# Two 3x3 convolutions by four products for two pixels, in a float32 stack of four layers with scans beside it

## The chip, the core and the metric

The kernel runs on one core of one Trainium2 chip, in one launch, in float32 throughout. The metric is the device time of one execution in microseconds (us). The profile is one execution taken by the hardware profiler; its engines are PE (TensorE matmul), PEld (its weight load), DVE (VectorE), ACT (ScalarE), POOL (GpSimd) and SP (SyncE, which issues all transfers here).

## What is computed

Eight images of 256 channels and 32 x 32 pixels go through four layers of the form x = x + layer(group_norm(x)), with a parameter-free group norm over 32 groups:

```
x = x + attention(gn(x))                      # 8 heads of 64, q and k of length one, projection
x = x + conv3x3(gn(x), s * sign_weights) + b1 # 256 -> 256 channels, padding 1
x = x + conv3x3(gn(x), weights) + b2          # 256 -> 256 channels, padding 1
x = x + layer3(gn(x))
```

Layer 3 is long: a layer norm, four branches of a selective scan (64 channels each, 128 inner channels, 16 states, 1024 tokens), a gate, depthwise convolutions along the tokens with pointwise ones after them, a second attention (8 heads of 32, "mixer attention"), a layer norm with gelu, a depthwise 3x3 convolution, another layer norm and a projection.

The change concerns the two 3x3 convolutions: out[o, h, w] is the sum over c, dy, dx of weight[o, c, dy, dx] times in[c, h + dy - 1, w + dx - 1].

## The kernel before

**Tiles.** An image is held as two tiles of 128 channels by 1024 pixels. A matmul takes 128 input channels by up to 512 pixels, and writes 512 float32 columns of PSUM. A float32 matmul appears in the profile as two records.

**Stages of one image.** `front_attention` (L576) is the first layer's attention; `front_convs` (L750) has its output projection and then the two convolutions; `scan_layers` (L1000) is the scan of layer 3; `back_layers` (L1151) has the layers up to and with the mixer attention; `back_out` (L1237) and `back_end` (L1263) close the image.

**The convolution.** `conv3x3` (L716) takes the statistics of the group norm (`group_stats`, L256, a chain of small operations between TensorE and VectorE), writes the normalised image into two tiles of 34 x 34 pixels with a border of zeros (`im`, by ScalarE), and for each of two output tiles m runs over input tile c, row dy, column dx and the two halves of the image: 36 matmuls into one PSUM tile of 1024 columns, each reading a shifted window of `im`. The weights come from memory in 12 chunks of 192 KB a convolution, through a pool of six buffers (`wsp`). One VectorE operation (`evac_1`, L763, or `evac_2`, L770) adds the PSUM tile to `xt`, and `channel_stats` (L249) takes the statistics for the next norm.

**The scan.** `scan_steps` (L885) works in 64 units an image: 4 branches, 2 halves of the tokens, 4 groups of states, 2 groups of channels. A unit has a product on GpSimd (`drive`, L929, tile `hs`), two exponentials on ScalarE into PSUM (`decays`, L933, tile `da`), two scans on VectorE (`scan`, L943), a second product on GpSimd (`weigh`, L958), and after each second unit eight records of small matmuls that add up the result (`add_up`, L965, tile `y`): I call two units that end so a pair, 32 an image. Before each branch, `branch_front` (L784) makes the branch's inputs, with TensorE, ScalarE, VectorE and a round trip through memory; `branch_back` (L857) closes it.

**The order.** [...]The order is written out by hand. Iteration b of the main loop has a *dense* stream, made of the back layers of image b-1 and the front layers of image b+1, and the *scans* of image b. Each stream is a generator that yields costs, planned TensorE time; `interleave` (L1335) adds up the dense costs, and takes one step of the scans (two steps are a unit) each time that a due time is reached, which then moves on by a pace:

```
spent += cost or 0.0
while scans is not None and due <= spent:
    due += pace
    with held():
        if next(scans, END) is END:
...
PACE = [1.8] + [2.95] * (batch - 2) + [1.6]
```

`Paced` (L93) and `held` (L118) tie each scan instruction to the last dense one of its engine, so that this order holds. `slow` (L1358) multiplies the costs of the front attention by 0.35, so few scan steps fall beside it. In the middle iterations the dense stream is: back layers with the mixer attention, output projections, front attention, then the convolutions of image b+1 with the closing layers of image b-1 between their steps (`amid`, L1348). Image 0's front layers stand alone ahead of the loop, and the last image's back layers alone behind it.

Of the kernel before, what the change touches and what calls it, by code (L numbers as in the profile page):

```python
# [2 lines left out]

# [1 line left out]

# [6 lines left out]
F32 = mybir.dt.float32  # L12
I32 = mybir.dt.int32
AF = mybir.ActivationFunctionType
ALU = mybir.AluOpType
# [4 lines left out]
P = 128  # L20
C = 256
N = 1024
HALF = 512
HALVES = (slice(0, HALF), slice(HALF, N))
NKT = N // P
TW = 34 * 34
NB, DM, DS, DTR = 4, 64, 16, 4


# [4 lines left out]
def preact_stack(ctx: ExitStack, tc: tile.TileContext, I, out, cols):  # L34
# [23 lines left out]
    ps_da = ctx.enter_context(tc.tile_pool(name="ps_da", bufs=2, space=PSUM))  # L58
    ps_y = ctx.enter_context(tc.tile_pool(name="ps_y", bufs=1, space=PSUM))
    dp = ctx.enter_context(tc.tile_pool(name="dp", bufs=2, space=DRAM))  # L60
    xdp = ctx.enter_context(tc.tile_pool(name="xdp", bufs=3, space=DRAM))

    def work(name):
# [5 lines left out]
    def big_tile():  # L69
        return ps_big.tile([P, N], F32, tag="big", name="big")  # L70
# [147 lines left out]
        half_qb, vec[:, cols["qpwb"] : cols["qpwb"] + 2], 0.5  # L218
    )


    images = [wp.tile([P, TW], F32, name="im%d" % t) for t in range(2)]
    raw = wp.tile([P, N + 4], F32, name="raw")
    for t in images + [raw]:
        nc.gpsimd.memset(t, 0.0)
# [19 lines left out]
    def stats_tile():  # L245

        return sp.tile([P, 2, 2], F32, tag="mv", name="mv", bufs=4)
# [8 lines left out]
    def group_stats(mv, psum):  # L256

        with urgent():
            pg = psum()
            tensor.matmul(  # L260
                pg[:, 0:4], gmat, mv.rearrange("p a b -> p (a b)"), start=True, stop=True
            )
            g = sp.tile([P, 2, 2], F32, tag="g", name="g", bufs=4)
            vector.tensor_copy(g.rearrange("p a b -> p (a b)"), pg[:, 0:4])
            d = sp.tile([P, 2], F32, tag="d", name="d")
            vector.tensor_sub(d, mv[:, :, 0], g[:, :, 0])
            vector.tensor_mul(d, d, d)
            pd = psum()
            tensor.matmul(pd[:, 0:2], gmat, d, start=True, stop=True)
            rs = sp.tile([P, 2], F32, tag="rs", name="rs", bufs=4)  # L270
            vector.scalar_tensor_tensor(
                rs, pd[:, 0:2], 1e-5, g[:, :, 1], ALU.add, ALU.add
            )
            inverse_root(rs)
            shift = sp.tile([P, 2], F32, tag="shift", name="shift", bufs=4)
            vector.scalar_tensor_tensor(
                shift, g[:, :, 0], -1.0, rs, ALU.mult, ALU.mult
            )
        return rs, shift

    def group_norm(xt, stats, dsts, view=lambda a: a):
        with urgent():
            scale, shift = stats
            for t in range(2):
                scalar.activation(
                    dsts[t],
                    view(xt[:, t]),
                    AF.Identity,
                    bias=shift[:, t : t + 1],
                    scale=scale[:, t : t + 1],  # L290
                )
# [421 lines left out]
    def image(a):  # L713
        return a.rearrange("p (h w) -> p h w", w=32)

    def conv3x3(xt, mv, name, bname, evac):  # L716


        im = [t.rearrange("p (h w) -> p h w", w=34) for t in images]
        group_norm(  # L720
            xt, group_stats(mv, acc_tile), [t[:, 1:33, 1:33] for t in im], image
        )
        mv = stats_tile()
        for m in range(2):
            scalar.activation(xt[:, m], xt[:, m], AF.Identity, bias=col(bname, m))
        yield 1
        for m in range(2):
            ps = big_tile()
            n = 0
            for c in range(2):  # L730
                for dy in range(3):
                    w = chunk(name, (m * 2 + c) * 3 + dy)
                    for dx in range(3):
                        for h in range(2):
                            tensor.matmul(
                                image(ps[:, HALVES[h]]),
                                w[:, dx],
                                im[c][:, 16 * h + dy : 16 * h + dy + 16, dx : dx + 32],
                                start=n == 0,
                                stop=n == 17,  # L740
                            )
                        n += 1
                    if n < 18:
                        yield 5.2
            evac(m, ps)
            channel_stats(mv, m, xt[:, m])
            yield 5.2
        return mv

    def front_convs(img):  # L750

        xt, o = img["x"], img.pop("o")
        mv = stats_tile()

        def evac_out(m, ps):
            vector.scalar_tensor_tensor(
                xt[:, m], ps, col("b_out", m), xt[:, m], ALU.add, ALU.add
            )
            channel_stats(mv, m, xt[:, m])

        yield from project_both("wout", o, evac_out)

        def evac_1(m, ps):  # L763
            vector.scalar_tensor_tensor(
                xt[:, m], ps, col("s1", m), xt[:, m], ALU.mult, ALU.add
            )

        mv = yield from conv3x3(xt, mv, "wc1", "b1", evac_1)

        def evac_2(m, ps):  # L770
            vector.tensor_add(xt[:, m], xt[:, m], ps)

        img["mv"] = yield from conv3x3(xt, mv, "wc2", "b2", evac_2)

# [580 lines left out]
            yield cost  # L1355
        yield from other

    def slow(stream):  # L1358

        for cost in stream:  # L1360
            yield SLOW * cost

    SLOW = 0.35
    PACE = [1.8] + [2.95] * (batch - 2) + [1.6]
    imgs = [{} for _ in range(batch)]
    drain(front_attention(image_of(0), imgs[0]), front_convs(imgs[0]))
    for b in range(batch):

        def dense():
            last = imgs[b - 1] if b > 0 else None  # L1370
            front = None
            if b + 1 < batch:
                front = front_attention(image_of(b + 1), imgs[b + 1])
            if last is None:
                yield from front
                yield from front_convs(imgs[b + 1])
                return
            for n, cost in enumerate(back_layers(last, begin=front)):
                yield cost
                if n == 2 and front is not None:  # L1380
                    next(front)
            if front is None:
                yield from back_out(last)
                yield from back_end(last, out[b - 1])
                return
            yield from islice(front, 4)
            ending = back_out(last)
            yield from islice(ending, 2)
            yield next(front)
            yield from ending  # L1390
            yield from slow(front)
            yield from amid(
                front_convs(imgs[b + 1]),
                back_end(last, out[b - 1]),
                (0, 4, 6, 7, 8, 9, 10, 11, 12, 13, 14, 16, 17, 20, 22, 25),
            )

        interleave(dense(), scan_layers(imgs[b]), PACE[b])
    last = imgs[batch - 1]
# [131 lines left out]
```

## Time and profile before

The time is 6625.64 us, the median of three (6609.48 to 6631.33). The profiled execution has a span of 6630.4 us.

| stretch | from, to (us) | what runs |
|---|---|---|
| image 0's front | 0 to 395 | attention, then two convolutions, no scans |
| iteration 0 | 395 to 1007 | front of image 1, scans of image 0 |
| iterations 1 to 6 | 1007 to 5668, about 777 each | back of b-1, front of b+1, scans of b |
| iteration 7 | 5668 to 6298 | back of image 6, scans of image 7 |
| the end | 6298 to 6630 | back of image 7 |

Costliest groups of instructions, with the mean time of a single record:

| engine, what | records | busy us | mean ns |
|---|---|---|---|
| PE, values of both attentions (acc<-p,v) | 4096 | 1189.7 | 653 |
| PE, the convolutions (big<-im,w) | 2304 | 1073.7 | 622 |
| POOL, drive (hs<-du,bc) | 512 | 1319.8 | 2594 |
| POOL, weigh (hs<-hs,bc) | 512 | 1278.8 | 2498 |
| DVE, scans | 1024 | 1228.2 | 1207 to 1268 |
| DVE, sums of the front attention (p<-p) | 448 | 717.0 | 1600 |

A row of groups reads: line, engine, operation, written tile <- read tiles, shapes, count | busy time, mean of one | idle time of the engine just before, and what ended most of it. Matmuls are pipelined, so the mean of one record is longer than what each adds to the engine's busy time. The line is mostly that of a helper (L101), so that groups are told apart by their tiles.

### The profile page before, as it was taken

What the parts mean: (1) busy time and instruction counts of PE and PEld (TensorE: products, weight loads), DVE (VectorE), ACT (ScalarE), POOL (GpSimd) and SP (SyncE); (2) the same over time, 40 slices, a digit from 0 to 9 for tenths busy, and PEclk for the clock granted to TensorE, in tenths of its full rate; (3) what the DMA queues carried; (4) which work ended last, traced back from release to release, by engine and by line L of the source; (5) the groups of instructions that cost most, each with busy time, mean ns of one, the idle gap of its engine ahead of it and who ended that gap; (6) DMA issues with size and microseconds to landing.
All of it is one profiled execution on the core that took longest, in us unless ns stands there. A gap on an engine that the chain in (4) does not pass through costs nothing.

```text
span 6630.4 us, 52730 instructions
## 1 busy us (share of the span) xinstructions
PE 5708.6 (86%) x17602; PEld 1926.6 (29%) x17602; DVE 3903.6 (59%) x4613; ACT 2687.2 (41%) x3225; POOL 2684.8 (40%) x1295
## 2 busy tenths in 40 slices
PE   8887689897998979998899989999799988978596
PEld 2331133222422234222332223222342223311222
DVE  4248745577465775567655675557755676455522
ACT  4134424553254532544245432555235442344242
POOL 0016662634355251642526334462526426176300
PEclk9988888998998989899999989899899999867697
DMA  1022332322233122331223222241213212233200
GB/s 41 27 60 79 77 90 73 101 60 65 74 97 91 48 69 76 88 83 52 76 78 92 70 64 80 72 110 45 79 59 105 79 53 80 65 94 89 58 21 26
DMA packets 217969, 471.36 MB, mean 71 GB/s; under 512 B 60244, under 2 KB 103636, under 8 KB 215640
## 3 DMA queue, kind: packets, MB, share of 16 engines
q1 hardware_dynamic: 217688, 467.90, 25.4%
q8 instruction: 141, 2.31, 0.1%
q14 instruction: 140, 1.15, 0.1%
HBM read 395.36 MB, written 63.96 MB: 69 GB/s over the span
## 4 chain that ended last, share of the span: by engine, by line
PE 53%; DVE 25%; DMA 6%; issue 6%; ACT 5%; POOL 4%; SPq 1%; POOLq 0%; DVEq 0%; ACTq 0%
PE big L101 34%; PE acc L101 12%; DVE hs L101 5%; PE da L101 4%; DVE p L101 3%; PE y L101 2%; DVE u L101 2%; DVE dw L101 2%; POOL hs L963 2%; POOL hs L931 2%; DVE t L101 1%; DVE dt L101 1%; DMA du_m<-a 1%; DVE st L101 1%; ACT p L101 1%
## 5 line engine op out<-in xcount | busy, mean ns | idle before, releaser
L931 POOL TENSOR_TENSOR hs<-du,bc 128x1024 f32<-128x1024 f32 x512 | 1319.8, 2594 | 1912.6 <-DMA du<-du_m 767.4
L963 POOL TENSOR_TENSOR hs<-hs,bc 128x1024 f32<-128x1024 f32 x512 | 1278.8, 2498 | 693.2 <-DVE hs L101 480.4
L101 ACT ACTIVATE p<-big 128x1024 f32<-128x1024 f32 x1024 | 1036.1, 1019 | 769.3 <-PE big L101 764.8
L101 PE MATMUL acc<-p,v 128*64 128x512 f32 x4096 | 1189.7, 653 | 2.6 <-ACT o L101 2.6
L101 PE MATMUL big<-im,w 128*128 128x512 f32 x2304 | 1073.7, 622 | 120.9 <-ACT im L101 102.6
L101 ACT ACTIVATE da<-dt,a_neg 128x512 f32<-128x512 f32 x1024 | 688.7, 687 | 791.3 <-DVE hs L101 484.3
L101 DVE TENSOR_TENSOR p<-p 128x1024 f32<-128x1024 f32 x448 | 717.0, 1600 | 273.7 <-ACT p L101 183.9
L101 DVE TENSOR_TENSOR_SCAN hs<-da,carry,hs 128x512 f32<-128x512 f32 x512 | 628.2, 1268 | 382.8 <-POOL hs L931 301.2
L101 DVE TENSOR_TENSOR_SCAN hs<-da,hs 128x512 f32<-128x512 f32 x512 | 600.0, 1207 | 256.8 <-ACT da L101 166.3
L101 PE MATMUL big<-q,k 64*128 64x512 f32 x2048 | 602.5, 657 | 76.7 <-ACT p L101 47.8
L101 PE MATMUL big<-qk,qk 32*128 32x512 f32 x2048 | 658.2, 687 | 9.2 <-ACT p L101 6.5
L101 PEld LDWEIGHTS big<-im,w 128*128 128x128 f32 x2304 | 445.4, 198 | 752.0 <-issue 613.8
L101 PE MATMUL y<-hs,sel 128*32 128x512 f32 x2048 | 410.9, 676 | 210.9 <-POOL hs L963 180.8
L962 POOL COPY carry<-hs 128x2 f32<-128x2 f32 x256 | 97.5, 381 | 947.6 <-DVE hs L101 928.2
L101 PEld LDWEIGHTS acc<-p,v 128*64 128x64 f32 x4096 | 217.6, 140 | 843.2 <-issue 759.8
L101 PEld LDWEIGHTS big<-qk,qk 32*128 32x128 f32 x2048 | 173.8, 195 | 487.2 <-issue 269.2
L101 PEld LDWEIGHTS big<-q,k 64*128 64x128 f32 x2048 | 161.2, 188 | 503.0 <-issue 247.4
L101 PE MATMUL big<-o,w 128*128 128x512 f32 x384 | 196.2, 664 | 92.6 <-DVE o L101 92.6
L101 PE MATMUL big<-xn,w 128*128 128x512 f32 x512 | 232.4, 608 | 5.6 <-ACT p L101 5.6
L101 DVE SCALAR_TENSOR_TENSOR dw<-xo,vec,dw 128x961 f32<-128x961 f32 (+1 forms) x128 | 194.1, 1550 | 29.3 <-ACT dw L101 29.1
L101 DVE SCALAR_TENSOR_TENSOR u<-raw,vec,u 128x1024 f32<-128x1024 f32 x96 | 153.9, 1603 | 87.2 <-ACT u L101 86.7
L101 DVE SCALAR_TENSOR_TENSOR xt<-big,vec,xt 128x1024 f32<-128x1024 f32 x48 | 61.4, 1279 | 236.2 <-PE big L101 236.2
(191 smaller groups left out, 5231.1 us busy)
## 6 DMA issues: line engine op xcount, KB each, us to landing
bc<-bc SPq DMA_DIRECT2D x1024, 128.0 KB
dt<-dt_m SPq DMA_DIRECT2D x512, 128.0 KB
du<-du_m SPq DMA_DIRECT2D x512, 128.0 KB
w<-in_wc SPq DMA_DIRECT2D x192, 192.0 KB
rs<-inv SPq DMA_DIRECT2D x64, 256.0 KB
dt_m<-dt SPq DMA_DIRECT2D x64, 256.0 KB
du_m<-a SPq DMA_DIRECT2D x64, 256.0 KB
xt<-in_x SPq DMA_DIRECT2D x8, 1024.0 KB
```

The source lines that it names most:

```text
L101: made = issue(*args, **kwargs)
L931: nc.gpsimd.tensor_mul(u["hs"], u["du"], both_groups(u["bc"][:, 0]))
L962: nc.gpsimd.tensor_copy(carry[:, u["q"], g : g + 2], hs[:, :, HALF - 1])
L963: nc.gpsimd.tensor_mul(hs, hs, both_groups(u["bc"][:, 1]))
```

## The change

For one row of three taps g0, g1, g2 and four neighbouring inputs x0 to x3, two neighbouring outputs need six products. They can be had from four:

```
y0 = (x0 - x2) g0 + (x1 + x2) (g0 + g1 + g2)/2 + (x2 - x1) (g0 - g1 + g2)/2
y1 = (x1 + x2) (g0 + g1 + g2)/2 - (x2 - x1) (g0 - g1 + g2)/2 - (x1 - x3) g2
```

The change does this along each row of the image, with the sum over channels and dy left to the matmuls:

- *Images.* `im` becomes 32 rows of 34. VectorE makes four transformed tiles of 512 columns (16 in each row) for each of the two input tiles, with strided reads (`d`, from the work pool, named `pos`).
- *Products.* Each output tile m has two PSUM tiles, one by one (`half`), each with two products of 512 columns. A half takes 3 dy x 2 input tiles x 2 products = 12 matmuls, so a convolution has 48 in place of 72. There is no border of rows above and below any more: dy = 0 and 2 work on 496 columns of the 512.
- *Evacuation.* Each half adds its products to the even and odd pixels of `xt` by three VectorE operations of 512 elements, strided by two, in place of one of 1024 for the whole tile.
- *Weights.* `transformed` makes the four weight sets of both convolutions once, in 12 blocks beside image 0's front attention (places 4, 6, ... 26 of its steps): two loads, two ScalarE copies, four VectorE operations and two stores to memory a block. All images then load chunks of 256 KB from there.
- *Pace.* A convolution step now yields 3.4 in place of 5.2. PACE becomes 1.65, 2.45 (six times) and 1.6; the front attention's costs are multiplied by 0.45 in place of 0.35, and those of the convolutions with the closing layers by 0.6, where they counted whole before.

```diff
+    def transformed(name):
+        u_d = wdp.tile([12, P, HALF], F32, tag=name, name="u_" + name)
+        wu[name] = u_d
+        for m in range(2):
+            for dy in range(3):
+                g, u = work("g_w")[:, 0 : 6 * P], work("u_w")[:, 0 : 8 * P]
...
+                for c in range(2):
+                    nc.sync.dma_start(out=g[:, c], in_=I[name][(m * 2 + c) * 3 + dy])
+                scalar.copy(u[:, 0, :, 0], g[:, :, 0])
+                scalar.copy(u[:, 1, :, 1], g[:, :, 2])
...
+                vector.tensor_add(half, g[:, :, 0], g[:, :, 2])
+                vector.tensor_scalar_mul(half, half, 0.5)
+                for at, sign in ((u[:, 0, :, 1], 0.5), (u[:, 1, :, 0], -0.5)):
+                    vector.scalar_tensor_tensor(
+                        at, g[:, :, 1], sign, half, ALU.mult, ALU.add
+                    )
+                for h in range(2):
+                    nc.sync.dma_start(
...
     def conv3x3(xt, mv, name, bname, evac):
...
+        d = [[work("pos")[:, 0:N] for _ in range(2)] for _ in range(2)]
+        for half, k, func, i, j in (
+            (0, 0, ALU.subtract, 0, 2),
+            (0, 1, ALU.add, 1, 2),
+            (1, 0, ALU.subtract, 2, 1),
+            (1, 1, ALU.subtract, 1, 3),
+        ):
+            for c in range(2):
+                vector.tensor_tensor(
+                    d[c][half][:, HALVES[k]].rearrange("p (h w) -> p h w", w=16),
+                    im[c][:, :, i : i + 31 : 2],
+                    im[c][:, :, j : j + 31 : 2],
+                    func,
+                )
...
-            ps = big_tile()
-            n = 0
-            for c in range(2):
-                for dy in range(3):
-                    w = chunk(name, (m * 2 + c) * 3 + dy)
-                    for dx in range(3):
-                        for h in range(2):
...
-                    if n < 18:
-                        yield 5.2
-            evac(m, ps)
-            channel_stats(mv, m, xt[:, m])
-            yield 5.2
+            for half in range(2):
+                ps = big_tile()
+                for n, dy in enumerate((1, 0, 2)):
+                    w = wsp.tile([P, HALF], F32, tag="w", name="w")
+                    nc.sync.dma_start(out=w, in_=wu[name][(m * 2 + half) * 3 + dy])
...
+                    for c in range(2):
+                        for k in range(2):
                             tensor.matmul(
...
+                    if n < 2:
+                        yield 3.4
+                evac(m, half, ps)
+                if half == 1:
+                    channel_stats(mv, m, xt[:, m])
+                yield 3.4
...
-    SLOW = 0.35
-    PACE = [1.8] + [2.95] * (batch - 2) + [1.6]
+    PACE = [1.65] + [2.45] * (batch - 2) + [1.6]
...
-    drain(front_attention(image_of(0), imgs[0]), front_convs(imgs[0]))
+    weights = chain(transformed("wc1"), transformed("wc2"))
+    drain(
+        amid(front_attention(image_of(0), imgs[0]), weights, range(4, 28, 2)),
+        front_convs(imgs[0]),
+    )
...
-            yield from slow(front)
-            yield from amid(
+            yield from paced(front, 0.45)
+            rest = amid(
...
+            yield from paced(rest, 0.6)
```

## The prediction

> **What bounds the kernel now.** The page comes first: parts 1 and 2 say which engine is nearest to full.
>
> ```profile
> PE 5708.6 (86%) x17602; PEld 1926.6 (29%) x17602; DVE 3903.6 (59%) x4613; ACT 2687.2 (41%) x3225; POOL 2684.8 (40%) x1295
> PEclk9988888998998989899999989899899999867697
> ```
>
> TensorE is busy for 86% of the span, and its granted clock lies below full speed in most slices. Part 5 gives the convolution its price.
>
> ```profile
> L101 PE MATMUL big<-im,w 128*128 128x512 f32 x2304 | 1073.7, 622 | 120.9 <-ACT im L101 102.6
> ```
>
> A float32 matmul stands in the records as two, so 2304 records are 1152 matmuls (8 images, 2 convolutions, 72 each), and one costs 1073.7/1152 = 0.93 us of TensorE. In the critical chain, 144 records with nothing beside them take 63.56 us: 0.883 us a matmul.
>
> An average over all stages can't tell what a saved matmul is worth, so I cut one image's period (image 2, 781 us, one of six nearly equal periods) into its stages, in the view of busy time by stretch (span, then busy time of PE, PEld, DVE, ACT, POOL, then clock).
>
> ```profile
> 1781.00:1868.00 87.00, 80.91 (x220) 36.60 (x218) 58.45 (x100) 33.80 (x36) 0.00 (x0) 0.90 0.22 70
> 1868.00:2060.00 192.00, 176.02 (x633) 41.74 (x632) 102.82 (x98) 117.97 (x144) 129.84 (x67) 0.90 0.35 92
> 2060.00:2124.00 64.00, 52.96 (x136) 20.10 (x134) 37.68 (x42) 20.13 (x28) 35.22 (x15) 0.92 0.35 97
> 2124.00:2303.00 179.00, 172.36 (x637) 46.25 (x636) 134.54 (x140) 99.91 (x120) 51.84 (x27) 0.99 0.21 55
> 2303.00:2359.00 56.00, 32.32 (x101) 16.05 (x97) 39.72 (x58) 12.28 (x15) 16.08 (x6) 0.78 0.18 53
> 2359.00:2562.00 203.00, 180.96 (x484) 76.61 (x484) 118.99 (x138) 51.02 (x63) 103.47 (x47) 0.91 0.28 79
> ```
>
> In order: the layers in front of the mixer, mixer attention, its output projections with the next image's values, front attention, projection and statistics, the two convolutions. TensorE is 89 to 96% busy in four of the six. The mixer row is the one to distrust: 192 us, where the last image's mixer attention, alone, takes 133 us (6366 to 6499).
>
> What runs beside it is the scan, in pairs of units that end in one group of y matmuls. Its fastest rhythm stands in the timeline:
>
> ```profile
> 1944.50 4.81 DVE L101 TENSOR_TENSOR_SCAN hs<-da,carry,hs 128x512 f32<-128x512 f32 x4 [4.85 <-POOL hs L931]
> ...
> 1947.10 4.69 POOL L963 TENSOR_TENSOR hs<-hs,bc 128x1024 f32<-128x1024 f32 x2 [0.32 <-DVE hs L101]
> 1951.76 4.67 POOL L931 TENSOR_TENSOR hs<-du,bc 128x1024 f32<-128x1024 f32 x2
> ```
>
> GpSimd works without a pause and gives one pair in 9.6 us. With branch changes and loads the rhythm is slower. Where scans are densest, in the last image's iteration, 23 pairs stand among the mixer's scores and take 349 us (5760 to 6109): 15.2 us a pair, with PE only 278 us busy at clock 0.72.
>
> **What the Trainium skill says.** "TensorE: Matmul & The Clock Gate", Part 1, What's actually happening: after an idle window TensorE falls to half rate. The trace agrees: after a gap of 2.08 us at 1986 us, a group that takes 1.13 us takes 2.08. So a stall for a scan costs more than itself. "SBUF — State Buffer", SBUF: two separate sides: a VectorE operation with two SBUF inputs and a GpSimd operation exclude each other for the whole instruction. The additions p<-p have a median of 1226 ns and a maximum of 3374. "VectorE: DVE Perf Modes", the errata section, prices a float32 tensor_tensor of 512 elements at 691 ns; this trace has 684 for xn<-xn,da. The stride of two in the new operands is in no trace row; I take 0.69 us, from 0.65 (half of 1.3 for the 992-element windows) to 0.9 (half of 1.79 for the 961-element ones).
>
> **The change, part by part.**
>
> *Matmuls.* Per convolution 72 become 48, and two thirds of those are 496 columns instead of 512. At 0.875 us (12 records in 5.25 us back to back) this is 63.0 to 48 × 0.875 − 32 × 0.027 = 41.1 us: 21.9 us less, 44 an image. It lies on the path wherever TensorE sets it.
>
> *Added VectorE work.* Eight differences or sums (two SBUF inputs) and twelve evacuations of 512 in place of two of 1.28 us: 8 × 0.69 + 12 × 0.69 − 2.56 = 11.2 us per convolution, 22 an image, on an engine that is 119 of 203 us busy in that stage. Most of it hides under matmuls. Not hidden are the first transforms: the chain statistics, image, first matmul leaves TensorE idle about 9 us (298.6 to 307.6) and now has a transform, a wait for the second half image, and a second transform in it: +2 us, and +0.8 us for the last three evacuations. Queued behind them on VectorE are scans and the depthwise convolution of the image before, and the next matmul group waits for the evacuations, with two PSUM buffers and a group every 10 us: I take 5 us an image more, from 0 to 15. Together +11 an image.
>
> *Weights on chip.* 12 blocks of 192 KB twice in, 256 KB twice out, some 1.4 us of VectorE and two short ScalarE copies each, beside image 0's attention, where VectorE is 106 of 210 us busy. In-order queues behind loads, and two of twelve work tiles held: +10 us, from 0 to 30, once. Each convolution then reads 12 × 256 KB instead of 12 × 192; in 41 us this is 75 GB/s, and the trace moves up to 110 GB/s in a slice, and six chunks are loaded ahead of the matmuls that hide them, so I cost it at nothing in the middle images.
>
> *Scans moved.* This is the part that the diff doesn't show. In the built programs' order on TensorE, of 32 pairs an image, the mixer's scores have 11 before and 14 after, the stretch to front attention 4 and 5, front attention 4 and 6, the convolutions 11 and 5 (two more before them, either way). Costs by stage, an image:
> - layers in front: a scan chain that starts a little earlier in TensorE's order, +1 (0 to 3).
> - mixer attention: TensorE's own need is 133 us plus 3.2 us a pair (2.1 for y, 1.1 for the branches' matmuls). Before: 133 + 11 × 3.2 = 168, measured 189 for the scores. After: 178, with the same 21 us of stalls 199; at the densest rhythm seen 14 × 15.2 = 213. I take 207: +18 (10 to 24).
> - stretch to front attention: one pair more, +3.
> - front attention: two pairs, 6.4 us of TensorE, and 19 us more of GpSimd against the additions of p: +8 (6 to 14).
> - projection and statistics: +1.
> - convolutions: −44, −5 pairs of y alone (−11), +11: −44 (−34 to −55).
>
> Sum −13 an image, −78 for six.
>
> *First and last.* Image 0 alone (0 to 395): −44 + 6 for two chains + 10 for the weights: −28. Iteration 0 (395 to 1007) runs at the scans' rhythm: PE 464 of 612 us. 16 pairs in front attention take 315 us (19.7 each), 18 after at TensorE's 3.2 to 19.7 us extra: +6 to +39, I take +25. Its convolutions, 262 us with 16 pairs, keep 14 pairs × 14.1 (226 us of scanning by 16) = 197 plus 20 of lead and tail: −45. Together −20. The last iteration and the drain (1.6 pace, no convolution) don't change.
>
> 6625.6 − 78 − 28 − 20 = **6500 us**.
>
> **The rivals.**
> *TensorE keeps all of it.* The scans fit into the denser stages for no more than y and branches: mixer +10, front +6, stretch +3, convolutions −55: −36 × 6 − 38 − 45 = −299: 6330 us. For it: 176 of 192 us busy in the mixer row; in such a stage the order of scans costs only their matmuls. Against it: the 15.2 us a pair in the last iteration.
> *The scans become the bound of the mixer.* Pairs cost what they cost now, 189/11 = 17.2 us, whatever stands between them: 14 × 17.2 = 241, +52; front attention +14, stretch +6, layers +3, convolutions −44: +31 × 6 = +186, −28, iteration 0 at nothing: 6785 us, slower. For it: 17.2 and 15.2 are close although one has half the dense work between. Against it: TensorE would then have to idle in a stage where now it hardly does.
> *The convolutions are bound by their chains.* Statistics, transforms and the previous image's closing norms on VectorE give back half: −20 instead of −44: +11 × 6 − 28 − 10 = 6650 us, no gain. Against it: the closing layers alone take 95 us (6535 to 6630), well below the stage.
>
> **How the numbers follow.** Forecast 0.45; TensorE keeps it 0.27; scans bound 0.13; chains bound 0.15. The forecast's own bounds (mixer and front ±8, chains ±10, six times) run from about 6390 to 6590. The range goes to just under the first rival and past the chains: 6300 to 6670; outside lie most of the scans' rival and a little of the first. Faster: 0.27 + 0.43 + a fifth of the chains = 0.73; same 0.07; slower 0.20.
>
> **What would show it.** Conv matmuls of 48 a convolution, near 82 us an image, and the stage at about 159 us instead of 203. The mixer stage near 210 us, with TensorE's busy share lower and waits for hs longer; 241 would mean the scans' rival, 200 the first. Idle TensorE before the first conv matmul near 12 us instead of 9 in image 0. VectorE busier by some 200 us in all. I'd be wrong if waits for weights from memory appear in the convolutions, or if image 0's attention grows by more than 30 us.

## Result: slower, and the profile after

The changed kernel takes 6871.59 us (median of four, 6847.25 to 6882.27), the kernel before 6624.91 us beside it. The ratio is 1.0371 with an interval of 1.0337 to 1.0404. I had forecast 6500 us, and the time lies above the range of 6300 to 6670.

The matmuls did go away. First, parts 1, 2 and 5 of the page of the changed kernel, with the lines that answer to those of before:

```profile
PE 5692.5 (83%) x16834; PEld 1849.9 (27%) x16834; DVE 4175.4 (61%) x4950; ACT 2683.2 (39%) x3249; POOL 2723.1 (40%) x1295
PEclk9988787798878978798887988779887897867697
...
L101 PE MATMUL big<-pos,w 128*128 128x496 f32 (+1 forms) x1536 | 723.0, 627 | 125.6 <-issue 108.5
```

The convolutions' matmuls fell from 2304 records and 1073.7 us to 1536 and 723.0: 350.7 us, or 21.9 us for each of 16 convolutions, as forecast. Yet TensorE is busy for 5692.5 us, against 5708.6 before. Something else on it became longer by nearly all that was saved. The clock row shows what: it has more 7s. Summed over the run, the trace grants TensorE half rate for 2175 us, against 1432 before. A matmul at half rate counts as busy for nearly twice as long (2.08 us in place of 1.13 for the same group, below), so the busy share hides the loss.

The same image (image 2) cut into the six stages of the prediction, in the view of busy time by stretch (span, then busy time of PE, PEld, DVE, ACT, POOL, then granted clock, DMA share, GB/s):

```profile
1803.00:1891.00 88.00, 81.01 (x221) 36.33 (x220) 59.48 (x102) 36.38 (x39) 1.30 (x1) 0.90 0.23 72
1891.00:2135.00 244.00, 218.51 (x665) 49.47 (x666) 126.19 (x116) 127.80 (x158) 158.82 (x80) 0.78 0.30 80
2135.00:2208.00 73.00, 58.83 (x152) 21.47 (x148) 46.13 (x52) 23.89 (x33) 45.18 (x26) 0.91 0.40 107
2208.00:2411.00 203.00, 180.38 (x645) 46.99 (x644) 154.15 (x150) 102.95 (x125) 80.98 (x32) 0.94 0.23 66
2411.00:2464.00 53.00, 32.70 (x99) 16.35 (x98) 33.87 (x53) 13.25 (x17) 17.21 (x11) 0.77 0.29 80
2464.00:2625.00 161.00, 128.56 (x332) 57.62 (x331) 107.75 (x139) 28.78 (x32) 39.08 (x15) 0.83 0.19 57
```

The convolutions (last row) went from 203 to 161 us. The mixer attention (second row) went from 192 to 244, at clock 0.78 instead of 0.90, with TensorE still 90% busy. The front attention (fourth) went from 179 to 203.

The mean of each stage over the six middle images, cut at the first and last matmul of each kind in the trace; "half" is time at half rate:

| stage | before, us | after, us | difference | half before, after | forecast |
|---|---|---|---|---|---|
| layers in front of the mixer | 87.4 | 88.2 | +0.8 | | +1 |
| mixer attention | 186.9 | 246.3 | +59.4 | 38.7, 114.9 | +18 |
| stretch | 66.5 | 74.6 | +8.1 | | +3 |
| front attention | 176.7 | 198.5 | +21.8 | 3.4, 19.9 | +8 |
| projection and statistics | 58.1 | 56.0 | -2.1 | | +1 |
| convolutions | 201.3 | 160.9 | -40.4 | 32.4, 52.3 | -44 |
| one image | 776.9 | 824.6 | +47.7 | | -13 |

Image 0's front went from 385.1 to 361.3 us (forecast -28, measured -23.8), iteration 0 from 621.9 to 607.3 (forecast -20, measured -14.6), iteration 7 and the end together took 2.5 us more. So 6 x 47.7 - 23.8 - 14.6 + 2.5 = 250 us, which is the difference of the two profiled spans (6880.5 and 6630.4).

What happens in the mixer stands in its timeline (start, duration, engine, operation; in brackets the idle time before it and what ended it). TensorE:

```profile
1962.83 1.13 PE L101 MATMUL big<-qk,qk 32*128 32x512 f32 x4
1963.89 1.08 PE L101 MATMUL acc<-p,v 128*64 128x512 f32 x4
1970.98 2.08 PE L101 MATMUL big<-qk,qk 32*128 32x512 f32 x4 [6.01 <-ACT p L101]
1972.98 1.98 PE L101 MATMUL acc<-p,v 128*64 128x512 f32 x4
...
1998.12 1.98 PE L101 MATMUL acc<-p,v 128*64 128x512 f32 x4
2000.03 1.94 PE L101 MATMUL y<-hs,sel 128*32 128x512 f32 x8
2001.89 1.25 PE L101 MATMUL big<-qk,qk 32*128 32x512 f32 x4
2003.07 1.08 PE L101 MATMUL acc<-p,v 128*64 128x512 f32 x4
```

A stall of 6.0 us, and after it every group takes 2.08 and 1.98 us instead of 1.13 and 1.08, for 31 us of work without a pause. The stall costs 6 us and the half rate behind it about 15. The other three engines tell where the stall comes from:

```profile
1962.34 7.93 POOL L993 TENSOR_TENSOR hs<-du,bc 128x1024 f32<-128x1024 f32 x3
1964.71 1.28 DVE L101 TENSOR_TENSOR_SCAN hs<-da,carry,hs 128x512 f32<-128x512 f32 x1 [4.55 <-POOL hs L993]
1966.03 0.69 ACT L101 ACTIVATE da<-dt,a_neg 128x512 f32<-128x512 f32 x1 [4.40 <-DVE hs L101]
1969.29 0.69 ACT L101 ACTIVATE da<-dt,a_neg 128x512 f32<-128x512 f32 x1 [2.57 <-DVE hs L101]
1969.92 1.92 ACT L101 ACTIVATE p<-big 128x1024 f32<-128x1024 f32 x2
```

GpSimd's product comes late, VectorE's scan waits for it, ScalarE's next `decays` wait for the scan's buffer, and the exponential of the attention's scores (`p<-big`) comes behind them on ScalarE: it starts at 1969.92, though TensorE had finished its last scores at 1963.96. TensorE waits for `p`.

### The profile page after: what moved, and what is told of

Its sections match the earlier page's. It is cut to its first block, busy times and chain, and to the rows that moved or that the text cites. A ratio compares the mean times of both kernels' runs of the same rounds, so it can differ in the third digit from the quotient of the medians.

```text
span 6880.5 us, 51771 instructions
## 1 busy us (share of the span) xinstructions
PE 5692.5 (83%) x16834; PEld 1849.9 (27%) x16834; DVE 4175.4 (61%) x4950; ACT 2683.2 (39%) x3249; POOL 2723.1 (40%) x1295
## 4 chain that ended last, share of the span: by engine, by line
PE 49%; DVE 25%; issue 8%; DMA 6%; ACT 5%; POOL 4%; SPq 2%; DVEq 0%; POOLq 0%; ACTq 0%
PE big L101 30%; PE acc L101 12%; DVE hs L101 6%; PE da L101 5%; DVE p L101 4%; PE y L101 3%; DVE dw L101 3%; POOL hs L993 2%; DVE u L101 2%; POOL hs L1025 2%; DMA dt<-dt_m 1%; ACT p L101 1%; DVE st L101 1%; ACT da L101 1%; DVE xt L101 1%
## 5 line engine op out<-in xcount | busy, mean ns | idle before, releaser
L1025 POOL TENSOR_TENSOR hs<-hs,bc 128x1024 f32<-128x1024 f32 x512 | 1315.5, 2570 | 1300.4 <-DVE hs L101 1107.8
L101 PE MATMUL acc<-p,v 128*64 128x512 f32 x4096 | 1302.6, 695 | 10.7 <-ACT both L101 9.6
L101 DVE TENSOR_TENSOR p<-p 128x1024 f32<-128x1024 f32 x448 | 753.0, 1681 | 291.0 <-ACT p L101 167.6
L101 DVE TENSOR_TENSOR_SCAN hs<-da,carry,hs 128x512 f32<-128x512 f32 x512 | 628.9, 1267 | 483.1 <-ACT da L101 254.2
L101 PE MATMUL big<-pos,w 128*128 128x496 f32 (+1 forms) x1536 | 723.0, 627 | 125.6 <-issue 108.5
L101 PE MATMUL big<-qk,qk 32*128 32x512 f32 x2048 | 755.1, 769 | 52.0 <-ACT p L101 51.4
L101 PE MATMUL big<-q,k 64*128 64x512 f32 x2048 | 637.3, 686 | 111.6 <-ACT big L101 56.5
L101 PE MATMUL y<-hs,sel 128*32 128x512 f32 x2048 | 445.3, 735 | 270.8 <-POOL hs L1025 207.8
L101 PEld LDWEIGHTS big<-pos,w 128*128 128x128 f32 x1536 | 304.8, 204 | 542.4 <-issue 498.5
L1024 POOL COPY carry<-hs 128x2 f32<-128x2 f32 x256 | 101.6, 397 | 756.7 <-DVE hs L101 621.9
L101 PEld LDWEIGHTS y<-hs,sel 128*32 128x32 f32 x2048 | 55.7, 118 | 593.2 <-POOL hs L1025 344.1
L101 DVE SCALAR_TENSOR_TENSOR u<-raw,vec,u 128x1024 f32<-128x1024 f32 x96 | 183.9, 1916 | 29.4 <-ACT u L101 28.9
```

What stands on the lines that cost most here:

```text
L101: made = issue(*args, **kwargs)
L1024: nc.gpsimd.tensor_copy(carry[:, u["q"], g : g + 2], hs[:, :, HALF - 1])
L1025: nc.gpsimd.tensor_mul(hs, hs, both_groups(u["bc"][:, 1]))
```

## Experiments

Two explanations stood against each other at first: that the new places of the scans cost more than forecast while the products save what they should, or that the products save less than their matmuls. When the first held, the question became what the places cost: a fixed price for each pair, scans that come late, or TensorE's slow return to full rate after a stall.

"Old places" of the scans are those of the kernel before (of 32 pairs an image, 11, 4, 4, 2, 11 in mixer, stretch, front attention, projection, convolutions in TensorE's order); "new places" those of the changed kernel (14, 5, 6, 2, 5). All ratios are to the kernel before, run beside.

### The two halves of the change, one at a time

The products alone, with the old places:

```diff
-                        yield 3.4
+                        yield 5.2
-    PACE = [1.65] + [2.45] * (batch - 2) + [1.6]
+    PACE = [1.8] + [2.95] * (batch - 2) + [1.6]
-            yield from paced(front, 0.45)
+            yield from paced(front, 0.35)
-            yield from paced(rest, 0.6)
+            yield from paced(rest, 1.0)
```

> The four products with the scan steps placed as in the kernel before (a convolution step yields 5.2, paces 1.8, 2.95 and 1.6, front attention times 0.35, convolutions whole): 11, 4, 4 and 11 pairs beside mixer, stretch, front attention and convolutions again. Theory A (the moved scans cost the time, by stalls that also put TensorE to half rate; the products themselves gain): mixer scores near 189 us instead of 242, front attention near 177 instead of 200, convolutions 160 to 185 instead of 162 with the denser scans: some 6350 us, and time at half rate back near 1430 us instead of 2177. Theory B (the added VectorE work and the longer chains of the products cost it, whatever the pace): near 6870 us.

Measured: 6595.92 us, ratio 0.9944 (0.9928 to 0.9959): the loss is gone, but the gain that I expected of the products (6350 us) didn't come. The kernel before with only the new places (the same lines the other way):

> The kernel before (six products, 72 matmuls) with the new paces, multipliers and step cost, so that its scans stand in the places of the changed kernel. Theory A: mixer scores near 242 us, front attention near 200, convolutions 203 less some 15 for five pairs fewer: 6950 to 7100 us, time at half rate near 2150 us. Theory B: within 1% of 6625 us.

Measured: 6957.71 us, ratio 1.0492 (1.0444 to 1.0539). Stages in us, means over the six middle images:

| | matmuls a convolution | places | mixer | front attention | convolutions | one image |
|---|---|---|---|---|---|---|
| before | 72 | old | 186.9 | 176.7 | 201.3 | 776.9 |
| products alone | 48 | old | 185.2 | 176.7 | 200.9 | 775.1 |
| places alone | 72 | new | 242.1 | 198.9 | 178.7 | 829.4 |
| after | 48 | new | 246.3 | 198.5 | 160.9 | 824.6 |

The places alone cost the whole loss and more. With the old places the products gain nothing in a middle iteration; their 37 us of the medians (6632.9 beside it to 6595.9) are mostly the 22.3 us of image 0, where no scan runs. In the convolutions of that kernel, 96 matmuls take as long as 144 did. The view of busy time, and what TensorE waited for in that stretch (total us, times, longest):

```profile
2352.00:2553.00 201.00, 148.73 (x390) 61.68 (x391) 147.02 (x171) 49.40 (x62) 100.58 (x47) 0.80 0.29 85
```

```profile
PE y L101 <- POOL hs L1025: 24.6, 4, 9.9
PE da L101 <- DVE hs L101: 14.9, 2, 8.3
PE big L101 <- DVE pos L101: 13.1, 2, 12.4
```

TensorE is 149 us busy at clock 0.80, and waits for scans (hs) and for the transforms (pos). In the means of the six middle images, the matmuls of this stage would take 42 us less at full rate than in the kernel before, but TensorE idles for 52.4 us in place of 21.9 and loses 11 us more to half rate. With 11 pairs here the scans seem to set the end of this stage once its matmuls are fewer, which the next experiment tests. That is the reason to move them. The price is what they do where they go.

### Lighter scans

The second product of a unit on GpSimd works on 128 of its 1024 columns, so the result of the scan is left incomplete; all instructions stay in their order.

```diff
-            nc.gpsimd.tensor_mul(hs, hs, both_groups(u["bc"][:, 1]))
+            few = hs[:, :, 0:64]
+            by = u["bc"][:, 1, 0:64].unsqueeze(1).to_broadcast([P, 2, 64])
+            nc.gpsimd.tensor_mul(few, few, by)
```

On the changed kernel, on the kernel before, and on the products with the old places:

> The changed kernel with the second GpSimd product of a unit on 128 of its 1024 elements (it leaves 7/8 of the weighting by C out), about 0.4 instead of 2.35 us, with all instructions and waits in place. If GpSimd's share of the scan rhythm (9.6 us a pair) makes the stalls of the mixer stage, the scores fall from 242 us to about 200 and the whole to some 6550 us. If the stalls come from the order of queues (ScalarE's exponentials of the attention behind those of the scan, scans behind a branch's front on VectorE), less than a third of that: over 6750 us.

> The kernel before with the second GpSimd product of a unit on 128 of 1024 elements (7/8 of the weighting by C left out). The first two experiments left the period of an image at 777 and 775 us with six and four products at the old places of the scans, and at 829 and 825 at the new ones: it is set by the scans' rhythm, not by the matmuls (theory A), or the added VectorE work eats just what the matmuls save (theory B). Here A and B both expect a gain, since the rhythm gets lighter by some 2 us a pair, up to where TensorE's own need binds: 6200 to 6400 us.

> The four products at the old places of the scans, with the same short second GpSimd product. Theory A: with a lighter rhythm the saved matmuls show, the convolution stage falls clearly below that of the run beside it, and the whole is more than 120 us below it. Theory B: the VectorE work is all still there, and the two differ by no more than the 37 us that they differ with the full product.

Measured: 6411.07 us (ratio 0.9672, 0.9619 to 0.9726), 6331.42 us (0.9554, 0.9521 to 0.9586) and 6224.04 us (0.9392, 0.9359 to 0.9424). (Two executions each; the first lies below what either explanation expected.) GpSimd is about 40% busy in each of these kernels with full scans, and yet cutting one of its two products short takes off 460, 294 and 372 us. In the changed kernel the mixer falls from 246.3 to 219.9 us and the front attention from 198.5 to 180.7. With light scans the products gain 107 us at the old places (6331 to 6224) where they gained 37 with full ones, and their convolution stage is 171.3 us against 191.1. So the scans' chain is what the saved matmuls ran into, if not all of it (107 us is less than the 120 that I expected).

The edit doesn't act through the chain alone. VectorE is busy for 3907 us in place of 4175 in the changed kernel, for the same 4950 instructions: the additions p<-p of the front attention have a mean of 1485 ns instead of 1681, while the scans keep theirs (1268 and 1267). So part of the gain is VectorE operations that get shorter when GpSimd works less. How much of the 460 us that is was not separated; in the mixer, where VectorE is busy for 122 us in place of 126, it can't be much.

### More of the scans beside the front attention

```diff
-    PACE = [1.65] + [2.45] * (batch - 2) + [1.6]
+    PACE = [1.65] + [3.4] * (batch - 2) + [1.6]
-            yield from paced(front, 0.45)
+            yield from paced(front, 0.785)
-            yield from paced(rest, 0.6)
+            yield from paced(rest, 1.2)
```

This gives 9, 3, 8, 2 and 10 pairs.

> The four products with the scans moved the other way: 9 pairs beside the mixer's scores, 3 in the stretch, 8 beside front attention, 10 beside the convolutions (11, 4, 4, 11 before; 14, 5, 6, 5 in the changed kernel), by paces 3.4, 0.785 and 1.2. If a pair costs about 17 us where the scans set the rhythm (mixer, convolutions) and 11 us beside front attention, an image saves 4 x 17 less 4 x 11 us: some 6450 us. If every stage slows by 17 us for each pair it is given, 6600 us.

Measured: 6881.63 us, ratio 1.0386 (1.0358 to 1.0413); mixer 198.0, front attention 215.1, convolutions 189.1 us. Both expectations (6450 and 6600 us) were far too low. A mixer with 9 pairs took longer than one with 11 (186.9): no fixed price for a pair explains that. Its time at half rate was 75.1 us, against 38.7, though TensorE idled hardly more there (13.6 us, against 12.5). What counts is not how many scans stand there, but how often TensorE stalls and, above all, for how long it then stays slow.

### How long TensorE stays slow: the rows of the scores

The records of the clock have full or half rate, in windows of 3.41 us. For each spell of half rate in the six middle images I took the work without a pause (gaps below 0.35 us) that TensorE did within the spell until it ended. In the changed kernel the median is 3.4 us in the front attention (28 spells, up to 6.4) and 5.2 in the convolutions (19, up to 6.0), but 19.7 in the mixer attention (36 spells, up to 31.4; the expectation below has 20.5, by another count). What is peculiar to the mixer is in its rows above: its scores read 32 of the array's 128 rows (`32*128`), those of the front attention 64. So I let a score matmul read the 64 rows of two heads, with the same number and size of matmuls; the separation of the heads is left out of the computation.

```diff
-                "q": [qk[t][r, 0:N] for r in rows],
-                "k": [qk[2 + t][r, 0:N] for r in rows],
+                "q": [qk[t][e * 64 : e * 64 + 64, 0:N] for e in range(2)],
+                "k": [qk[2 + t][e * 64 : e * 64 + 64, 0:N] for e in range(2)],
```

> The changed kernel, but each score matmul of the mixer attention reads 64 rows of q and k (two heads together) in place of the 32 of its own head; the separation of the heads is left out of the computation, the number and size of the matmuls stay. Theory R (after a stall, TensorE gets its full rate back slowly because the mixer's scores fill only 32 of 128 rows): median time of work until the full rate is back in the mixer falls from 20.5 us to about 4 to 8, half-rate time there from 115 to about 45 us an image, the stage from 246 to 205-215 us, the total to about 6650 us. Rival S (the rate follows the stalls and how the queues interlock, whatever the rows): mixer within 5 us of 246, total 6820 to 6900 us.

Measured on the changed kernel: 6693.71 us, ratio 1.0076 (1.005 to 1.0102), so 178 us less. The median in the mixer fell from 19.7 to 5.3 us (40 spells, none above 9.4), half rate from 114.9 to 44.4 us an image, the mixer from 246.3 to 221.1; the other stages of a middle image stayed within 0.6 us. Its timeline has the same kind of stall with another end:

```profile
1916.84 1.08 PE L101 MATMUL acc<-p,v 128*64 128x512 f32 x4
1922.33 1.35 PE L101 MATMUL big<-qk,qk 64*128 64x512 f32 x4 [4.41 <-ACT p L101]
1923.60 1.98 PE L101 MATMUL acc<-p,v 128*64 128x512 f32 x4
1925.51 1.54 PE L101 MATMUL y<-hs,sel 128*32 128x512 f32 x8
1926.98 1.13 PE L101 MATMUL big<-qk,qk 64*128 64x512 f32 x4
```

4.4 us of waiting, and full rate again 4.7 us later. The number of spells didn't fall, only what follows each stall. The size of the gain was under what I had expected of it (about 6650 us, mixer 205 to 215): part of the time that the clock gave back became waiting (TensorE idles 33.5 us in the mixer instead of 26.2), so a second cause is left.

What ends a spell can be seen too. I cut the half-rate time of the middle mixers into the windows of 3.41 us, and kept those that TensorE filled with scores and values alone. In the changed kernel there are 91, and only one of them is the last of its spell; 34 of the 36 spells end in a window that has `y` matmuls in it, which read 128 rows, as the spell in the timeline of the result does at 2000.03. With 64 rows, all 23 such windows are the last of their spell. Over the nine kernels here with 32 rows it is 12 of 412 windows, over the five with 64 rows and no zeros 76 of 81. So with scores on 32 rows the full rate doesn't merely come late: scores and values alone hardly ever bring it, and TensorE stays slow until other matmuls come by. That also fits the run with 9 pairs, since fewer pairs bring fewer `y` groups, but no run varied this alone.

One thing isn't separated: with the rows, their place changed as well. A pair's two heads read neighbouring blocks of 32 rows before, and the two halves of the array after.

The same edit at the old places, on the kernel before, and on the kernel before with the new places:

> The same edit (64 rows for each score matmul of the mixer attention, separation of the heads left out) on the products with the old places of the scans, which took 6596 us. Theory R: half-rate time in the mixer from 30 to about 15 us an image, the stage from 185 to about 178, total 6530 to 6560 us. Rival S: no change, 6580 to 6620 us.

> The kernel before, with 64 rows for each score matmul of the mixer attention (separation of the heads left out, as in the two runs like it). It completes the table of rows against places. Half-rate time in the mixer before is 38.7 us an image, of which the rows should explain the part by which spells last longer than about 5 us: mixer 187 to about 179 us, iteration 7 630 to about 603, total 6540 to 6580 us, as for the products with the old places (6596 to 6546). If the few rows mattered only where stalls are as frequent as in the changed kernel, the total stays within 0.3% of 6632 us.

> The kernel before with only the new places of the scans (6958 us) and 64 rows for each score matmul of the mixer attention (separation of the heads left out). It closes the table of products, places and rows. If places and rows act without regard to the matmuls of the convolutions, the rows take 178 us off, as in the changed kernel (6872 to 6694): about 6780 us, mixer 242 to about 218 us; the places then still cost 200 us against 6577. If the cost of the places is the rows' alone, it comes near 6600 us.

Measured: 6546.26 us (0.9856, 0.9822 to 0.989), 6576.69 us (0.9937, 0.9915 to 0.9958) and 6801.64 us (1.0248, 1.0215 to 1.0281). With this the table of medians is full (us):

| | old places | new places | the places cost |
|---|---|---|---|
| 72 matmuls, 32 rows | 6624.9 | 6957.7 | 333 |
| 48 matmuls, 32 rows | 6595.9 | 6871.6 | 276 |
| 72 matmuls, 64 rows | 6576.7 | 6801.6 | 225 |
| 48 matmuls, 64 rows | 6546.3 | 6693.7 | 147 |

The slow return by few rows is a third of the places' cost with 72 matmuls (108 of 333) and nearly half with 48 (129 of 276). It was in the kernel before too, where it cost about 48 us. (The medians come from several sessions, in which the kernel before had 6621 to 6642 us, so 10 or 20 us in this table say little.)

### Are stalls and slow return two causes?

Both edits in the changed kernel, 64 rows and the short product (with what each leaves out):

> The changed kernel with both: 64 rows for each score matmul of the mixer attention (separation of the heads left out) and the second product of the scan on 128 of 1024 columns (so the scan's result is left incomplete). Each alone gave a mixer stage of 221 and 220 us in place of 246 (kernel before: 187). If two causes stand side by side, slow return to full rate by few rows, and TensorE waiting for scans that GpSimd makes late, both together give the mixer about 196 to 200 us and the total about 6250 to 6300 us. If both edits only cure the same loss (fewer stalls or shorter ones), the second adds little: mixer 212 to 220, total 6340 to 6400 us.

Measured: 6243.15 us, ratio 0.9407 (0.9377 to 0.9437). The mixer is 246.3 us in the changed kernel, 221.1 with 64 rows, 219.9 with the short product, and 200.0 with both: -25.2, -26.4 and -46.3. The two nearly add, so they are two causes. The mixer of one image in the view of busy time, first of the kernel with the short product alone, then with both:

```profile
1783.00:2005.00 222.00, 204.56 (x652) 47.13 (x652) 121.82 (x116) 126.78 (x157) 96.97 (x79) 0.82 0.35 91
```

```profile
1754.00:1954.00 200.00, 177.95 (x649) 43.32 (x648) 119.71 (x115) 125.90 (x157) 96.67 (x79) 0.94 0.37 96
```

PE's busy time falls by 27 us for nearly the same number of records, and the clock goes from 0.82 to 0.94. Something is left: 200.0 us are 13 above the kernel before as it is, and 24 above the kernel before with the same short product (176.4). About 10 us of that are the matmuls of three more pairs; and TensorE still idles for 22.1 us there, against 7.6 in the kernel before with the short product.

### Versions that beat both

The products with the old places, but with the changed kernel's pace in iteration 0, where no mixer attention runs:

```diff
-    PACE = [1.8] + [2.95] * (batch - 2) + [1.6]
+    PACE = [1.65] + [2.95] * (batch - 2) + [1.6]
+        STEP[0] = 3.4 if b == 0 else 5.2
...
-                        yield 5.2
+                        yield STEP[0]
```

> Products with the old places of the scans in iterations 1 to 7, but iteration 0 with the places of the changed kernel (pace 1.65, convolution steps of 3.4). If the places act on each iteration by itself, iteration 0 takes 607 us as in the changed kernel in place of 628, the periods stay at 775 and the total is 6575 us, which would beat both kernels. If iteration 0's gain is given back in iteration 1 (its scans start earlier but wait for the same back layers), the total stays at 6596 us.

Measured: 6571.34 us, ratio 0.9895 (0.986 to 0.9929). Iteration 0 took 608.7 us in place of 627.9, and nothing was given back later.

To that, 64 rows with the whole computation kept: the keys are held twice, each time with every second block of 32 rows set to zero, and a head reads its 32 rows and 32 of zeros.

```diff
+                qk[t] = [work("qk3"), work("qk3")]
+                for e in range(2):
+                    vector.tensor_scalar(
+                        qk[t][e][:, 0:N],
+                        ps,
+                        col("ain_b", t),
+                        mask[:, e : e + 1],
+                        ALU.add,
+                        ALU.mult,
+                    )
...
+            groups = [slice(e * 64, e * 64 + 64) for e in range(2)]
...
+                "q": [qk[t][r, 0:N] for r in groups],
+                "k": [qk[2 + t][s][r, 0:N] for r in groups],
+                "v": [v_of(4 * t + s), v_of(4 * t + s + 2)],
```

> The whole computation with 64 rows a score matmul: products, old places of the scans in iterations 1 to 7, new ones in iteration 0 (6571 us without the rows), and the keys of the mixer attention twice, each with the rows of every second block of 32 set to zero by a mask of one column, so that a head reads 64 rows of which 32 add nothing. Two more tiles live in the same 12. If zeros warm the engine like other data: 6571 - 50 + 5 for two more VectorE operations an image = about 6525 us, mixer half-rate time about 20 us an image. If the two tiles held make the front attention wait for its own: above 6571 us. If zero rows don't count for the clock: 6570 to 6590 us, with spells as long as before.

Measured: 6515.72 us, ratio 0.9845 (0.9824 to 0.9867), the fastest of the kernels that compute everything. Mixer 179.0 us, half rate 17.6 us an image; the median until full rate is 6.5 us (17 spells), and with the run below 18 of 23 windows of scores and values alone were the last of their spell. So rows with zeros in the keys count for the rate nearly like others. Its scores on the page, and below them those of the kernel without the mask, at the same places:

```profile
L101 PE MATMUL big<-qk,qk 64*128 64x512 f32 x2048 | 645.6, 662 | 18.1 <-DVE qk L101 12.1
```

```profile
L101 PE MATMUL big<-qk,qk 32*128 32x512 f32 x2048 | 640.1, 668 | 10.1 <-ACT p L101 7.5
```

The wider scores cost TensorE next to nothing (645.6 us against 640.1), and the stage gains by the clock: 184.9 us without the mask with 27.9 at half rate, 179.0 with it.

With one work tile more and one weight buffer less:

> The same with 13 work tiles, for which one of six weight buffers is given up. If the tiles held were what costs in the run beside it, this one is faster by as much; if a weight chunk then comes late in the convolutions (waits of TensorE for w, none now), it is slower. About 6525 us, within 15 of the run beside it, if neither binds.

Measured: 6541.91 us, ratio 0.9885 (0.9864 to 0.9907), 26 us behind. The layers in front of the mixer took 98.4 us in place of 85.5, and there TensorE waits for a weight:

```profile
PE big L101 <- DMA w<-in_ainqk: 10.1, 1, 10.1
```

The sixth weight buffer is worth more than a thirteenth tile, and the place where it shows is not the convolutions, where I looked for it.

## Why the prediction was wrong

*Matmuls: right.* 21.9 us a convolution forecast, 21.9 measured.

*Added VectorE work: right in price, short in sum.* The transforms, priced at 0.69 us with no row to go by, have a median of 0.68 us and a mean of 0.78 (100 us for 128). With the operations that add PSUM to `xt` (177.5 us, before 80.9, those of projections among both) this work grew by 197 us, against 16 x 11.2 = 179. In all VectorE is busy for 272 us more, where I had said some 200: operations that stood there before got longer too, p<-p by 36 us.

*Weights on chip and image 0: right.* -23.8 us for image 0, forecast -28 with 10 us for the weights. Waits of TensorE for the new weights came to 14.9 us in the whole run, against 18.3 for the old ones.

*Convolutions: right in the sum.* -40.4 against -44. Its parts were not: I gave the matmuls 44 us and the leaving scans 11, less 11 for the added work. The matmuls alone gave 0.4 us with the scans still there, the scans' leaving alone 22.6 (201.3 to 178.7), both 40.4. The saving needs the move, and that the sum agrees is luck.

*Mixer attention: wrong, and this is the step that failed.* I wrote that TensorE needs 133 us plus 3.2 a pair, added "the same 21 us of stalls" (199), and took 207 on the way to the densest rhythm's 213. Measured: 246. The term for the stalls was held constant and priced as idle time. The traces split the stage as follows, in us, means of the six middle images; the last column is half of the time in which TensorE worked at half rate:

| mixer attention | time | its matmuls at full rate | TensorE idle | lost to half rate |
|---|---|---|---|---|
| before | 186.9 | 157 | 12.5 | 17 |
| after | 246.3 | 167 | 26.2 | 53 |

So what I called 21 us of stalls was already 30, and it became 79: of the +59.4, 36 us are lost to half rate, 14 are idle, and about 10 are the added matmuls. The 21 came out too small because y was priced at 2.1 us a pair, where its eight records take 1.06 at full rate (at 1983.40 in the trace of before). I had quoted the mechanism myself, from the Trainium skill ("TensorE: Matmul & The Clock Gate", Part 1, What's actually happening), and shown one gap of 2.08 us with a group at double length after it. I did not look how long the slow time lasted: 17.1 us after that very gap (1989.6 to 2006.7). Nor did I ask how many more gaps three more pairs bring. The trace of before had 38.7 us of half rate an image in that stage, in three spells of up to 27.3 us, where the front attention has 3.4 us in one.

*Front attention and stretch: the mechanism right, the size too small.* +21.8 and +8.1 against +8 and +3. With the short product the front attention is 180.7 us, 6 above the kernel before with it (174.6), so most of it is GpSimd's products in the way, as forecast; 8 us of the 22 are half rate again.

*The rivals.* "The scans become the bound of the mixer" came near in numbers (mixer 241 forecast, 246 measured), and its image sum of +31 against +48. Its mechanism, a fixed 17.2 us a pair, fell with the run of 9 pairs in 198 us. I held against it that "TensorE would then have to idle in a stage where now it hardly does". It doesn't have to: it works at half rate, and the profile calls that busy. That argument took weight from the rival that came nearest. "TensorE keeps all of it" has no support left; "the convolutions are bound by their chains" comes near only at the old places, and there the chains are those of 11 pairs of scans, not the statistics and transforms that I had in mind.

Open is what decides, for a given placement, when TensorE stalls and when the next wide matmuls come: the mixer with 9 pairs had 75 us of half rate in 24 spells, that with 11 had 39 in 18. Which pair meets which queue was not worked out.

## What to carry to other kernels

A busy share near 90% doesn't say that an engine does 90% of its work. Multiply it by the granted clock of that stage: 0.90 x 0.78 = 0.70 for the mixer here, whose matmuls at full rate are 167 of 246 us. Price a stall with the half-rate time behind it, as long as this stage's own spells last. When work is moved out of a stage to free it, test the move alone, without the saving that it is to serve: here the move cost 333 us, and the saving gained 37 without it. Matmuls on few rows of the array that fill a long stretch can be worth widening with zeros if that stretch has stalls: here it took the time from 6571 to 6516 us.

## What the runs showed of the hardware

How soon TensorE is back at full rate depends on the rows that its matmuls read. The Trainium skill ("TensorE: Matmul & The Clock Gate", Part 1, What's actually happening) has the full rate back after one busy window of some 3.4 us. The front attention agrees, where scores on 64 rows alternate with values on 128: a median of 3.4 us of unbroken work. In the mixer attention, where scores on 32 rows alternate with the same values, it does not: 90 of 91 windows full of them were followed by half rate again, and the median is 19.7 us, up to 31.4. With 64 rows it is 5.3, and with the keys zero in 32 of these 64 it is 6.5. That the edit of the rows decides is shown by these runs; that the chip measures activity by the share of the array in use is only a guess that fits.

Nor does TensorE have to be idle for a whole window before it falls to half rate: the gap of 2.08 us that the prediction quotes is shorter than one. In 3 of the 18 spells of the mixer before, TensorE worked without a pause in the window just ahead of the half rate; each of these windows had matmuls on 4 rows in it (`da<-low,mdtw`).

The other surprise is a size: with GpSimd at 40% of the span, shortening one of its products was worth 4.5 to 6.7% of the time. An engine far from full can still set the rhythm, if other engines' queues carry its lateness to the engine that is nearly full.
